# Moving the copies and picks of one-group pairs ahead of the squares of the pair before them

## The chip, the cores and the metric

The kernel runs on one core of a Trainium2 chip. The core has five engines that work side by side, each through its own queue in order: TensorE (PE, matrix products; the loading of its weights is shown as PEld), VectorE (DVE), ScalarE (ACT), GpSimd (POOL) and SyncE (SP), which here only issues transfers. They wait for each other through semaphores. The metric is the time of one execution on the device in microseconds (us); several runs are given by their median.

## The reference

A graph of 6250 nodes (128 features) and 100000 edges, sorted by destination. For each edge the features of both ends and of the edge are multiplied by a weight, normalised over the 128 outputs, cut at zero, and summed by source node; the sums are added to the nodes and normalised again:

```python
row, col = edge_index[0], edge_index[1]            # src, dst
msg_in = jnp.concatenate([x[row], x[col], edge_attr], axis=-1)
h = msg_in @ W + b
mu = jnp.mean(h, axis=-1, keepdims=True)
var = jnp.mean(jnp.square(h - mu), axis=-1, keepdims=True)
h = (h - mu) * jax.lax.rsqrt(var + LN_EPS) * gamma + beta
out = jax.ops.segment_sum(jax.nn.relu(h), row, num_segments=x.shape[0])
x = _layernorm(x + out, axis=-1)
```

## The kernel before

The nodes are split into 50 blocks by source (source modulo 50), the edges, in tiles of 128, into six splits (`SPLITS`). Two kinds of work run side by side.

*Edge work* goes over 196 quads q of four tiles. `edges` puts the product of the edge features with the weight (L589, eight instructions) and the rows of the destination (L593, four) into a bank of PSUM named hp; `evict` copies it on ACT (L601, L602) into one of eight buffers hs; `scatters` sends each tile's rows on POOL, by one indirect transfer per tile (L619), to the place in DRAM (sorted) where the edges of one source block lie together. For most quads a scatter is tied to PE: it waits until PE has come to a given place of the next quad's work. SP loads what the edges need (eT, db, win).

*Block work* takes the rows of a split back from DRAM when all its scatters have landed. It goes by pairs of blocks (`Pair`). A pair of the first four splits has two groups of three or four tiles, a pair of the fifth split (25 pairs, here numbered 100 to 124, and the last split's blocks are not among them) has one group of four tiles. A pair's steps are:

- `load_pair` (SP, L673): its rows into one of four buffers hl.
- `ones` (DVE, L691): one-hots of the edges' source nodes, ohe.
- `turn` (PE, L703): four transposes of them into the one bank tr; `turned` (ACT, L707): their copy, ohn.
- `seed` (ACT, L713): a copy of the rows into one of three PSUM banks sel.
- `pick` (PE, L730): twelve products add the source nodes' share to that bank.
- `square` (ACT, L739, L742): four squares with their sums over a row, and the root of the variance.
- `root`, `scale` (DVE, L748, L754): the reciprocal and the scaled and cut message, msg, one of two buffers.
- `sums` (PE, L763): the sums by node into the one bank pa; `add` (DVE, L771): they are added to acc.

The last split is worked on in a *tail* of 14 units of one or two pairs each (class `Unit`, the same steps with lines L799 to L870, where the rows come into the bank by a product with the unit matrix, L818), followed by the last normalisation and the output. `Unit.load` (L792) waits for the last scatter.

The order of PE, DVE, ACT and SP is written out by hand: the order in which the program emits instructions is the order of each queue. POOL's is left to the planner. A pair starts every four steps of `work`; the list `FLOW` says at which step of a pair (its offset) each of its steps is emitted, and within one step of `work` the list's own order holds:

```python
    FLOW = [(14, lambda x: x.add()), (11, second(lambda x: (x.root(1), x.scale(1)))),
            (9, lambda x: (x.root(0), x.scale(0))), (13, lambda x: x.sums()),
            (8, second(lambda x: x.pick(1))), (6, lambda x: x.pick(0)),
            (7, second(lambda x: x.seed(1))), (5, lambda x: x.seed(0)),
            (9, second(lambda x: x.square(1))), (7, lambda x: x.square(0)),
            (4, lambda x: x.turned()), (2, lambda x: x.turn()),
            (0, lambda x: x.ones()),
            (-6, None)]
```

`second` skips a step for pairs of one group. So with i for the pair that started last, ACT's order among one-group pairs is turned, seed, square of pair i-1, then the same three of pair i. PE's is sums of i-3, picks of i-1, transposes of i. Per quad q the program emits edge loads, the one-hots of quad q + 2 (DVE, L577), the products of quad q, one step of `work`, the eviction of q, and the other steps that are due (for the fifth split's pairs 25 pairs over quads 181 to 196, six or seven steps per quad). The rest of the steps, mixed with the first unit, follows behind the loop.

Of the kernel before, what the change touches and what calls it, by code (L numbers as in the profile page):

```python
# [83 lines left out]
def fast_path(ctx, tc, io, bad_d):  # L84
# [584 lines left out]
    def load_pair(s, p):  # L669

        k = 2 * SPLITS[s][1]
        pair = late["blk"].tile([P, KMAX, ROW], F32, name="hl", bufs=4)
        nc.sync.dma_start(flat(pair[:, :k, :]),  # L673
                          dram_ap(sorted_d[s], p * k * P * ROW, [[k * ROW, P], [1, k * ROW]]))
        loaded[s, p] = pair
# [274 lines left out]
    first, second = pieces[0][1], pieces[1][1]  # L950
# [62 lines left out]
    def second(step):  # L1013
        return lambda x: step(x) if len(x.groups) > 1 else None

    FLOW = [(14, lambda x: x.add()), (11, second(lambda x: (x.root(1), x.scale(1)))),
            (9, lambda x: (x.root(0), x.scale(0))), (13, lambda x: x.sums()),
            (8, second(lambda x: x.pick(1))), (6, lambda x: x.pick(0)),
            (7, second(lambda x: x.seed(1))), (5, lambda x: x.seed(0)),
            (9, second(lambda x: x.square(1))), (7, lambda x: x.square(0)),  # L1020
            (4, lambda x: x.turned()), (2, lambda x: x.turn()),
            (0, lambda x: x.ones()),
            (-6, None)]

    def work(n):

        nonlocal n_steps
        for _ in range(n):
            for off, step in FLOW:
                i = n_steps - LEAD - off  # L1030
                if i % 4 or not 0 <= i // 4 < len(pairs):
                    continue
                if step is None:
                    load_pair(*pairs[i // 4])
                    continue
                if off == 0:
                    at_work[i // 4] = Pair(*pairs[i // 4])
                step(at_work[i // 4])
            n_steps += 1
# [66 lines left out]
    units = [Unit(sum(sizes[:i]), n) for i, n in enumerate(sizes)]  # L1106
# [45 lines left out]
    work(n_tail - n_steps)  # L1152
    for i in range(3):
        units[i].load()
    work(2)
    units[3].load()
    units[0].ones()
    work(2)
    units[0].turn()
    units[0].turned()  # L1160
    work(3)
    units[0].pick(0)
    units[1].ones()
    units[0].xs_load()
    units[1].turn()
    units[0].square()
    work(4)
    assert not steps_at and not others and all(cleared[s] == NB // 2 for s in cleared)
    units[2].ones()
    units[4].load()  # L1170
# [6 lines left out]
@with_exitstack  # L1177
def gnn_resnorm_kernel(ctx, tc, io):
    nc = tc.nc
    keep = ctx.enter_context(tc.tile_pool(name="keep", bufs=1))  # L1180
    bad_t = keep.tile([1, 1], I32, name="bad_t")
    with ExitStack() as inner:
        fast_path(inner, tc, io, bad_t)
    flag = nc.values_load(bad_t[0:1, 0:1], min_val=0, max_val=1 << 20,
                          skip_runtime_bounds_check_because="a sum of small counts")
    with tc.If(flag > 0):
        with ExitStack() as inner:
            general_path(inner, tc, io)
# [233 lines left out]
```

## Time and profile before

| what | us |
|---|---|
| median of 3 runs (lowest, highest) | 1142.15 (1140.5, 1145.27) |
| the profiled execution | 1144.18 |
| its span, first to last instruction | 1142.4 |
| busy in it: PE, PEld | 874.6, 811.4 |
| busy: DVE, ACT, POOL | 841.6, 768.3, 817.1 |
| one-hot copies of one-group pairs (L707), first to last | 955.12 to 1041.42 |
| last scatter starts | 1032.22 |
| the tail's first load; unit 1's first product | 1035.83; 1049.23 |

In the rows that are shown, a line of the order of time has the start, the duration, the engine, the line of the program, the operation, what it writes and reads by the program's names, how many instructions are put together, and in brackets how long the engine had been idle and who released it. A row of the waits has who waited for whom, microseconds in total, how many times, and the longest. A row of a stage has its bounds and length, the busy time of PE, PEld, DVE, ACT and POOL with their counts, the granted clock of TensorE as a share of full speed, the share of the DMA engines, and GB/s. Matmuls are pipelined, so a group's duration reaches beyond the start of the next; the distances between starts say what a step costs PE.

### The profile page before, as it was taken

The page shows a single profiled execution, that of the slowest core. Times are in us where ns is not written, and L with a number is a line of the kernel's source. Part 1 is how long each engine was busy: PE and PEld are TensorE (multiplying, and loading weights), DVE is VectorE, ACT ScalarE, POOL GpSimd, SP SyncE. Part 2 cuts the span into 40 slices and gives each one's busy share as a digit, 9 for nine tenths or more (in the row PEclk, how much of TensorE's full clock was granted, in tenths as well). Part 3 has the DMA queues.
Part 4 walks back from the last instruction along what each step waited for, and adds up shares of the span by engine and source line. Part 5 has one row for each costly group of instructions (what it writes and reads, how often), then busy time and mean ns, then how long its engine had stood idle before and what let it go on. Part 6 is the DMA issues. An engine that isn't in the chain of part 4 may idle for free.

```text
span 1142.4 us, 27577 instructions
## 1 busy us (share of the span) xinstructions
PE 874.6 (77%) x8873; PEld 811.4 (71%) x8873; DVE 841.6 (74%) x2352; ACT 768.3 (67%) x3115; POOL 817.1 (72%) x877
## 2 busy tenths in 40 slices
PE   3668676537887869787787879888888998777993
PEld 2657565437787868787787869888887888775762
DVE  6875666236877777676868678987989887666984
ACT  3324432207676867677676778988889998776993
POOL 3677777777777777777777777777777776761675
PEclk9688887667988989899899989999999999999996
DMA  7698998457877763887786758776878676744531
GB/s 216 208 274 255 293 290 250 133 175 230 254 255 231 241 202 124 281 244 237 226 262 208 228 185 283 250 228 211 254 225 259 202 236 183 209 127 139 166 131 59
DMA packets 123539, 247.48 MB, mean 217 GB/s; under 512 B 47036, under 2 KB 55245, under 8 KB 123384
## 3 DMA queue, kind: packets, MB, share of 16 engines
q1 hardware_dynamic: 97332, 191.92, 55.0%
q0 software_dynamic: 25184, 53.31, 13.2%
q8 instruction: 71, 1.16, 0.4%
q14 instruction: 84, 0.69, 0.2%
q10 hardware_dynamic: 868, 0.40, 0.2%
HBM read 155.74 MB, written 89.80 MB: 215 GB/s over the span
## 4 chain that ended last, share of the span: by engine, by line
PE 31%; DVE 22%; DMA 22%; ACT 13%; issue 6%; POOL 4%; SPq 1%; ACTq 0%; POOLq 0%; DVEq 0%
DMA sorted<-hs,place_i 16%; PE pa L763 7%; PE sel L730 7%; PE hp L589 7%; DVE msg L754 5%; DMA db<-drel_d 4%; ACT sq L739 3%; DVE sc L437 3%; PE beside L484 3%; ACT sel L713 3%; DVE ohe L691 3%; ACT ohn L707 2%; POOL sorted L619 2%; ACT hs L601 2%; PE hp L593 2%
## 5 line engine op out<-in xcount | busy, mean ns | idle before, releaser
L619 POOL DMA_INDIRECT sorted<-hs,place_i x782 | 757.8, 969 | 253.6 <-issue 102.7
L730 PE MATMUL sel<-xa,ohn 128*128 128x128 bf16 x2550 | 188.1, 225 | 126.5 <-ACT sel L713 125.5
L730 PEld LDWEIGHTS <-ohn 128*128 128x128 bf16 x2550 | 165.4, 101 | 141.4 <-issue 111.4
L589 PE MATMUL hp<-w,eT 128*128 128x128 f32 x1564 | 241.5, 303 | 26.4 <-ACT hs L601 26.4
L739 ACT ACTIVATE sq<-sel 128x128 f32<-128x128 f32 x850 | 224.2, 281 | 47.4 <-PE sel L730 47.4
L589 PEld LDWEIGHTS hp<-w,eT 128*128 128x128 f32 x1564 | 218.8, 214 | 52.3 <-ACT hs L601 28.9
L754 DVE SCALAR_TENSOR_TENSOR msg<-sel,rstd,cut 128x128 f32<-128x128 f32 x850 | 240.7, 345 | 7.9
L601 ACT COPY hs<-hp 128x512 f32<-128x512 f32 x196 | 114.1, 582 | 195.3 <-DMA sorted<-hs,place_i 152.5
L763 PE MATMUL pa<-msg,ohe 128*128 128x130 f32 x1700 | 234.0, 291 | 3.5 <-DVE msg L754 3.0
L763 PEld LDWEIGHTS pa<-msg,ohe 128*128 128x128 f32 x1700 | 214.8, 203 | 5.3 <-DVE msg L754 4.3
L739 ACT ACTIVATION_READ_ACCUMULATOR sq<-sel 128x1 f32 x850 | 179.8, 212 | 0.0
L691 DVE TENSOR_TENSOR ohe<-hl,beside 128x1024 f32<-128x1024 f32 (+2 forms) x125 | 131.6, 1053 | 36.2 <-DMA hl<-sorted 24.5
L713 ACT COPY sel<-hl 128x512 f32<-128x512 f32 (+1 forms) x225 | 127.9, 568 | 14.4 <-DVE msg L754 14.1
L577 DVE TENSOR_SCALAR ohd<-db,part_w 128x512 bf16<-128x512 bf16 x194 | 72.1, 372 | 66.1 <-DMA db<-drel_d 41.3
L707 ACT COPY ohn<-tr 128x1024 bf16<-128x1024 bf16 (+2 forms) x125 | 108.7, 870 | 0.0
L748 DVE RECIPROCAL rstd<-std 128x4 f32<-128x4 f32 (+1 forms) x225 | 38.7, 172 | 91.1 <-ACT std L742 88.1
L593 PE MATMUL hp<-win,ohd 126*128 126x128 bf16 x782 | 82.9, 232 | 2.4 <-DMA win<-xb_d 2.4
L703 PE MATMUL tr<-ident_h,ohe 128*128 128x128 bf16 x850 | 70.4, 224 | 8.7 <-issue 7.4
L742 ACT ACTIVATE std<-ss,eps 128x4 f32<-128x4 f32 (+1 forms) x225 | 66.9, 297 | 7.3
L593 PEld LDWEIGHTS <-ohd 126*128 126x128 bf16 x782 | 66.7, 105 | 6.3 <-issue 2.6
L771 DVE TENSOR_TENSOR acc<-acc,pa 128x260 f32<-128x260 f32 x100 | 41.7, 417 | 29.4 <-PE pa L763 26.6
L703 PEld LDWEIGHTS <-ohe 128*128 128x128 bf16 x850 | 54.6, 100 | 9.4 <-issue 7.6
(193 smaller groups left out, 1038.6 us busy)
## 6 DMA issues: line engine op xcount, KB each, us to landing
eT<-in_eT SPq DMA_DIRECT2D x96, 512.0 KB
hl<-sorted SPq DMA_DIRECT2D x75, 528.0 KB
db<-drel_d SPq DMA_DIRECT2D x96, 256.0 KB
sorted<-empty SPq DMA_DIRECT2D x100, 198.0 KB
hl<-sorted SPq DMA_DIRECT2D x50, 264.0 KB
sorted<-hs,place_i POOLq DMA_INDIRECT x782
hl<-sorted SPq DMA_DIRECT2D x25, 396.0 KB
sorted<-empty SPq DMA_DIRECT2D x50, 132.0 KB
```

Of the source, the lines that this page charges most:

```text
L589: pe(nc.tensor.matmul(hp[:, j, :], eT[:, at], w[:, 2, :], start=j == 0, stop=False, skip_group_check=True), 4)
L593: pe(nc.tensor.matmul(hp[:, j, :], oh[:3 * WN, at], win[:3 * WN, :], start=False, stop=j == m - 1, skip_group_check=True))
L601: nc.scalar.copy(hs[:, :m, 0:D], hp[:, :m, :])
L619: i = nc.gpsimd.indirect_dma_start(out=sorted_d[s][:, :], out_offset=bass.IndirectOffsetOnAxis(ap=place_i[:parts, t:t + 1], axis=0), in_=h ...
L691: nc.vector.tensor_tensor(self.ohe[:, :k, :], self.hl[:, :k, D:D + 1].to_broadcast([P, k, P]), row_bc(iota_p, k), op=ALU.is_equal)
L703: pe(nc.tensor.transpose(tr[:, j, :], half[:, j0 + j, 1::2], ident_h))
L707: nc.scalar.copy(self.ohn[:, :self.k, :], self.tr[:, :self.k, :])
L713: nc.scalar.copy(self.sel[g][:, :m, :], self.hl[:, j0:j0 + m, 0:D])
L730: pe(nc.tensor.matmul(sel[:, j, :], self.ohn[:, j0 + j, :], xa[:, b, i * D:(i + 1) * D], start=False, stop=j == m - 1 and i == 2, skip_gro ...
L739: nc.scalar.activation(sq[:, j, :], self.sel[g][:, j, :], AF.Square, accum_out=ss[:, j:j + 1])
L754: nc.vector.scalar_tensor_tensor(self.msg[:, j0 + j, 0:D], self.sel[g][:, j, :], rstd[:, j:j + 1], cut, op0=ALU.mult, op1=ALU.max)
L763: pe(nc.tensor.matmul(self.pa[:, h, :], self.ohe[:, j, :], self.msg[:, j, :], start=(j == h), stop=(j == k - 2 + h)), 4)
```

## The change

For pairs with one group the copy of the one-hots and of the rows is emitted at step 3 of the pair instead of steps 4 and 5, in the list ahead of the squares (step 7, so those of the pair before fall into the same step of `work`), and its picks at step 5 instead of 6. Pairs with two groups keep their order. Behind the loop the last steps are mixed in another order with the first unit: its one-hots come one step sooner, its transposes and its copy stand ahead of the last pair's squares, its picks ahead of the last pair's scaling. Nothing else is changed.

```diff
+    def single(step):
+        return lambda x: step(x) if len(x.groups) == 1 else None
+
     FLOW = [(14, lambda x: x.add()), (11, second(lambda x: (x.root(1), x.scale(1)))),
             (9, lambda x: (x.root(0), x.scale(0))), (13, lambda x: x.sums()),
-            (8, second(lambda x: x.pick(1))), (6, lambda x: x.pick(0)),
-            (7, second(lambda x: x.seed(1))), (5, lambda x: x.seed(0)),
+            (8, second(lambda x: x.pick(1))), (6, second(lambda x: x.pick(0))),
+            (5, single(lambda x: x.pick(0))),
+            (7, second(lambda x: x.seed(1))), (5, second(lambda x: x.seed(0))),
+            (3, single(lambda x: (x.turned(), x.seed(0)))),
             (9, second(lambda x: x.square(1))), (7, lambda x: x.square(0)),
-            (4, lambda x: x.turned()), (2, lambda x: x.turn()),
+            (4, second(lambda x: x.turned())), (2, lambda x: x.turn()),
             (0, lambda x: x.ones()),
             (-6, None)]
...
     for i in range(3):
         units[i].load()
+    work(1)
+    units[0].ones()
+    units[3].load()
+    work(1)
+    units[0].turn()
+    work(1)
+    units[0].turned()
+    work(1)
+    units[0].pick(0)
+    units[0].xs_load()
+    units[1].ones()
     work(2)
-    units[3].load()
-    units[0].ones()
-    work(2)
-    units[0].turn()
-    units[0].turned()
-    work(3)
-    units[0].pick(0)
-    units[1].ones()
-    units[0].xs_load()
     units[1].turn()
     units[0].square()
-    work(4)
+    work(5)
...
     units[2].ones()
     units[4].load()
```

## The prediction

> **What bounds the kernel now.** I read the page's slices first, then busy time by stage, then the waits of the stage that the change touches, then one pair in order of time.
>
> ```profile
> span 1142.4 us, 27577 instructions
> ...
> POOL 3677777777777777777777777777777776761675
> ...
> 958.50:1024.40 65.90, 50.63 (x580) 48.06 (x579) 43.83 (x137) 50.74 (x228) 44.89 (x47) 1.00 0.58 173
> ...
> ACT sq L739 <- PE sel L730: 19.0, 23, 1.0
> ...
> 959.39 0.57 ACT L707 COPY ohn<-tr 128x512 bf16<-128x512 bf16 x1
> 1024.35 0.56 ACT L707 COPY ohn<-tr 128x512 bf16<-128x512 bf16 x1
> 1041.42 0.57 ACT L707 COPY ohn<-tr 128x512 bf16<-128x512 bf16 x1
> ```
>
> The slices (a fortieth of the span each) show POOL, which issues the scatters, at seven tenths in nearly every slice up to the 36th; towards its end the pairs with one group (25 of them, numbers 100 to 124) have their stretch. There no engine is full: in the stage row ACT is busy 50.74 of 65.90 us, PE 50.63, DVE 43.83, POOL 44.89. ACT's only wait in 958 to 1043 is the one quoted, 23 times before the first square, 19.0 us in all. The copies L707 of pairs 101, 119 and 124 stand at 959.39, 1024.35 and 1041.42: 23 periods in 82.03 us, of which the last five, without edges, take 3.41 each and the first eighteen 3.61. One period, with an eviction in it:
>
> ```profile
> 1002.69 0.57 ACT L707 COPY ohn<-tr 128x512 bf16<-128x512 bf16 x1
> 1003.16 0.59 ACT L601 COPY hs<-hp 128x512 f32<-128x512 f32 x1
> 1003.73 0.60 ACT L713 COPY sel<-hl 128x512 f32<-128x512 f32 x1
> 1004.38 0.83 PE L730 MATMUL sel<-xa,ohn 128*128 128x128 bf16 x12 [0.82 <-ACT sel L713]
> 1005.05 0.39 PE L703 MATMUL tr<-ident_h,ohe 128*128 128x128 bf16 x4
> 1005.27 1.11 PE L763 MATMUL pa<-msg,ohe 128*128 128x130 f32 x8
> 1005.31 0.28 ACT L739 ACTIVATE sq<-sel 128x128 f32<-128x128 f32 x1 [0.98 <-PE sel L730]
> 1006.22 1.05 PE L589 MATMUL hp<-w,eT 128*128 128x128 f32 x8
> 1006.69 0.57 ACT L707 COPY ohn<-tr 128x512 bf16<-128x512 bf16 x1
> 1006.81 0.18 DVE L748 RECIPROCAL rstd<-std 128x4 f32<-128x4 f32 x1 [1.73 <-ACT std L742]
> 1007.03 1.13 DVE L754 SCALAR_TENSOR_TENSOR msg<-sel,rstd,cut 128x128 f32<-128x128 f32 x4
> 1007.15 0.59 ACT L713 COPY sel<-hl 128x512 f32<-128x512 f32 x1
> 1007.67 0.59 ACT L601 COPY hs<-hp 128x512 f32<-128x512 f32 x1
> ...
> 1010.44 1.13 DVE L754 SCALAR_TENSOR_TENSOR msg<-sel,rstd,cut 128x128 f32<-128x128 f32 x4
> 1011.48 0.42 DVE L771 TENSOR_TENSOR acc<-acc,pa 128x260 f32<-128x260 f32 x1
> ```
>
> The chain is serial: copy of the one-hots (L707), copy of the rows (L713), picks on PE (L730), squares on ACT (L739), next copy. PE waits for ACT (0.82 before 1004.38), then ACT for PE (0.98 before 1005.31). An eviction (L601, 1003.16 to 1003.73) adds 0.57 when it stands between the copies and nothing when it stands behind the second (1007.67), since it falls into ACT's wait.
>
> **The change, part by part.** No instruction is added or removed; instructions change places.
>
> *1. The copies of pair i+1 ahead of the squares of pair i.* ACT's own work per pair, start to start, is 0.46 (1006.69 to 1007.15) + 0.52 (1007.15 to 1007.67) + 1.38 (1005.31 to 1006.69) = 2.36 us, against 3.41. The naive gain is 0.98 x 23, about 22 us. I don't take it, because the next wait is already in the order of PE's queue: sums (L763) of pair i-2, picks of pair i, transposes (L703) of pair i+1. That order stays, but the squares of i-2 now run behind the copies of i-1, directly ahead of the copies of i. So the sums that stand in front of the picks, and which had a full period of slack, are now late: they need the scaled messages (L754) and the bank that the add (L771) of the pair before empties, and DVE does that add behind the scaling. From the first square of pair i-1 to the first square of pair i+1, two periods, the loop is, start to start: square to reciprocal 1.50 (1005.31 to 1006.81); to scaling 0.22 (to 1007.03); to add 1.04 (1010.44 to 1011.48); to sums 0.46; to picks 0.95 (1005.27 to 1006.22, what followed the sums there); to transposes 0.67 (1004.38 to 1005.05); to the one-hot copy 0.43; to the row copy 0.46; to the square 0.52. The two links that those rows lack:
>
> ```profile
> 873.50 0.40 DVE L771 TENSOR_TENSOR acc<-acc,pa 128x260 f32<-128x260 f32 x1
> 873.96 1.89 PE L763 MATMUL pa<-msg,ohe 128*128 128x130 f32 x12 [0.36 <-DVE acc L771]
> ...
> 1047.82 0.62 PE L809 MATMUL tr<-ident_h,ohe 128*128 128x128 bf16 x8 [1.26 <-DVE ohe L799]
> 1048.48 1.01 ACT L812 COPY ohn<-tr 128x1024 bf16<-128x1024 bf16 x1 [0.41 <-PE tr L809]
> ```
>
> 873.50 to 873.96 is add to sums (PE waited for that add); the copy starts 0.04 behind the end of the transposes (1048.44), and four transposes take 0.39 (1005.05). Sum 6.25 us per two pairs, 3.13 per pair. In general, with d the time between the copies of two neighbouring pairs, the next d is the larger of 2.36 and 6.25 - d.
>
> Five periods without edges: 5 x 3.13 = 15.6 us. Two things cost nothing as long as their cover holds. The row copy of pair i+1 takes the bank (one of three) of pair i-2, whose scaling ends a period earlier; were it late, the squares would queue behind the copy on ACT. DVE's own work is about 2.4 per pair (one-hots, reciprocal, scaling, add, a part of a slot's edge one-hots), so it has 0.7 to spare.
>
> *2. Edges in that loop.* ACT's evictions now always fall between squares and the next copy: 2.36 + 0.57 = 2.93, under 3.13. The products of a slot cost PE 0.95 + 0.23 = 1.18:
>
> ```profile
> 1012.10 1.11 PE L589 MATMUL hp<-w,eT 128*128 128x128 f32 x8
> 1013.05 0.39 PE L593 MATMUL hp<-win,ohd 126*128 126x128 bf16 x4
> 1013.27 1.11 PE L763 MATMUL pa<-msg,ohe 128*128 128x130 f32 x8
> ```
>
> In ten of the twelve slots (edge quads 184 to 195, six or seven steps each) they stand between transposes and sums, where PE waits for the add; there they only demand d of at least 0.22 - 0.43 + 1.18 + 0.95 + 0.67 + 0.43 = 3.02. In two, 190 and 192, whose first step is two steps behind a pair's start, they stand between picks and transposes, inside the loop, and the eviction waits for them: PE's products end 0.67 + 0.95 + 0.39 behind the picks' start, then 0.04 and 0.57, so the copy comes 2.62 behind the picks where it came 1.10, 1.52 more. Stepping d with these rules from pair 101 gives 3.2, then 3.06 and 3.20 in turn up to pair 110, then 4.7, 2.37, 3.9, 3.9, 2.4, 3.8, 2.4, 3.8 to pair 119: 58.7 us for eighteen, where 18 x 3.13 would be 56.3. With part 1: 58.7 + 15.6 = 74.3 against 82.03, gain 7.7.
>
> *3. The beginning.* The first pair's picks had stood behind the products of 956.02, at 957.14; now they stand ahead of them, behind the sums of 954.62, so at 956.02 at the earliest (1.40 later, as the products did).
>
> ```profile
> 954.62 1.56 PE L763 MATMUL pa<-msg,ohe 128*128 128x130 f32 x12
> 956.02 1.05 PE L589 MATMUL hp<-w,eT 128*128 128x128 f32 x8
> 957.14 0.83 PE L730 MATMUL sel<-xa,ohn 128*128 128x128 bf16 x12
> ```
>
> The products then start at 956.7, the transposes at 957.9, the eviction (0.57) follows the products, and the copy of pair 101 comes at 958.5 for 959.39: gain 0.9. The row copy of pair 100 waits for a bank of pair 98 (scaled until 954.8): 0.4 us, hidden behind the same picks.
>
> *4. The tail's entry.* Unit 0's one-hots, transposes, copy and picks move ahead of the last pairs' scaling and squares. Measured from the copy of pair 124, before it is 7.81 us to unit 1's first matmul (1041.42 to 1049.23). After: sums of 122 and picks of 124 at 2.15, unit 0's transposes at 2.82, its copy at 3.3, squares of 124 at 3.75; DVE has unit 1's one-hots (1.22, from 4.2) ahead of that reciprocal, so the scaling starts at 5.6, the add 1.04 later, sums 0.46 later at 7.1, unit 1 at 8.05. Loss 0.2. This needs unit 0's one-hots on DVE (0.68) no later than 2.1 behind the copy, at about 1034.7, which hangs on the scatters:
>
> ```profile
> L619 POOL DMA_INDIRECT sorted<-hs,place_i x54: 867/965/992, 958.0 to 1032.2; - x54
> ...
> 1030.95 0.97 POOL L619 DMA_INDIRECT sorted<-hs,place_i  x1 [0.30 <-ACT sq L739]
> 1032.22 0.87 POOL L619 DMA_INDIRECT sorted<-hs,place_i  x1 [0.30 <-issue]
> 1035.83 7.47 SPq L792 DMA_DIRECT2D hl<-sorted  x7
> 1042.81 0.68 DVE L799 TENSOR_TENSOR ohe<-hl,beside 128x512 f32<-128x512 f32 x1
> 1049.23 1.02 PE L818 MATMUL sel<-hl,ident 128*128 128x512 f32 x2
> ...
> 670.95 0.34 SPq L673 DMA_DIRECT2D hl<-sorted  x1
> 675.21 1.22 DVE L691 TENSOR_TENSOR ohe<-hl,beside 128x1024 f32<-128x1024 f32 x1 [4.01 <-DMA hl<-sorted]
> ```
>
> Unit 0's load waits for the last scatter: 3.61 us from its start to the load. The 54 scatters from 958.0 run at 1.27 where nothing holds them (1030.95 to 1032.22); 53 x 1.27 = 67.3, so the last starts at 1025.3 at best, and I take 1026.5, since slots of 5.1 us (6.25 steps of a pair's four, at 3.25 per pair) just feed four scatters of 1.27. The load goes at 1030.1 and lands within 4.3 (670.95 to 675.21, for twice the bytes): 1034.4. It just fits. SP's loads wait for row copies, which all come earlier, and land two periods ahead of their use: nothing. Unit 1's transposes and unit 0's squares now stand behind the scaling of 124 on their queues' lists, and DVE, not they, is what unit 1 waits for: nothing.
>
> The tail behind unit 1 has the same instructions in the same order and moves as a whole.
>
> **Sum.** 0.9 + 7.7 - 0.2 = 8.4 us off. The profiled execution took 1144.18 (span 1142.4 and 1.8 around it), 2.03 above the median of 1142.15. So 1135.8 for such an execution, 1133.7 as a median. 0.5% of this kernel, 5.7 us, is about what a measurement can tell from no change.
>
> The Trainium skill's Perfetto Trace Analysis, section Engine Utilization, says that in a well-optimized kernel at least one engine should approach full utilization; by it the loop would close up to ACT's own work, which is the first rival below. The stage row, 50.74 of 65.90, doesn't show that yet.
>
> **Rivals.**
>
> *ACT alone bounds* (the sums don't hold the picks). For it: wherever sums follow at once (1005.27) DVE was done. Against it: PE did wait for the add at 873.96. Then pair 124 is through early and unit 0's rows decide: 1025.3 + 3.61 + 4.3 = 1033.2 for its one-hots, 9.6 ahead of 1042.81; that is 1142.15 - 9.6 = 1132.5, or 1131.5 if half the bytes land a us sooner. Chance 0.15.
>
> *The scatters don't come forward*: they are tied to PE's progress and POOL has little to spare. Then the one-hots come at 1035.83 + 4.3 = 1040.1, and unit 1 follows about 6.4 later as before (1042.81 to 1049.23), at 1046.5: 2.7 us gained, 1139.4. Each us of the last scatter later than 1026.5 costs one. For it: of the 74.2 us from the first of the 54 to the last, 67.3 are POOL's own pace. Against it: the other 6.9 are waits behind a PE that now runs ahead. Chance 0.2. The Trainium skill's SBUF — State Buffer, section SBUF: two separate sides, says that certain VectorE operations lock GpSimd out of a shared port so that it can't write descriptors; a denser DVE would then slow the scatters. Here they last 867 to 992 ns with DVE busy 43.83 of 65.90 us, which shows no such loss.
>
> *Slower: the products stand in the loop in every slot*, because they are held there (rows or windows of the edges late, or DVE's one-hots for them behind the new scaling). Its place is between picks and transposes, its price 1.52 per slot: 12 x 1.52 = 18.2 for the 2.4 counted, 15.8 more, 1149.5. It decides from a mean period of 3.57 (82.03 / 23), that is from some five more slots than my two. Against it: PE had no wait for edge data in this stretch. Chance 0.08.
>
> *The wait only moves* from squares to copies, the period stays about 3.4: 0 to 2 us gained, 1141. Chance 0.07.
>
> **How the numbers follow.** My forecast has 0.5; its own range is 1131.5 to 1136.5. The range of 1130.5 to 1140.5 takes in the second and third case and leaves out the slower one and half of the last. Faster by over 0.5% (below 1136.4): the ACT case and nearly all of the forecast, 0.64; within: the scatter case, the moved wait and the forecast's edge, 0.28; slower 0.08.
>
> **What would show it.** ACT's wait for picks falls from 19.0 us to under 5; in its place come waits of the one-hot copies for transposes, some 0.77 x 23 = 15 to 18 us, and of the sums for the add. The copies of 101 and 124 stand near 958.5 and 1032.8, the last scatter near 1026.5, unit 0's load near 1030, unit 1's first matmul near 1041, and from there to the end as many us as before. It is wrong if the mean period is under 2.9 or over 3.4, or if unit 0's one-hots wait for their rows.

## The result, and the profile after

The changed kernel takes 1136.28 us (median of 8 runs, 1132.87 to 1138.08), the kernel before beside it 1143.51 (8 runs, 1140.5 to 1146.59): a ratio of 0.993, 95% interval 0.991 to 0.995. That is 7.2 us off, inside the predicted range and 2.6 us above the predicted 1133.7. The profiled execution took 1132.87, the lowest of its eight, with a span of 1131.1.

Its page, the span and POOL's slices, and three stages (bounds and length; busy time and count of PE, PEld, DVE, ACT, POOL; clock; DMA share; GB/s): from the copy of pair 101 to that of 119, on to that of 124, and from unit 1's first product to the end.

```profile
span 1131.1 us, 27553 instructions
...
POOL 3677777777777777777777777777777776772675
```

```profile
955.20:1014.30 59.10, 50.03 (x570) 46.70 (x569) 42.77 (x138) 50.09 (x222) 44.33 (x46) 1.00 0.63 192
1014.30:1029.70 15.40, 10.80 (x126) 9.73 (x125) 10.21 (x33) 12.48 (x58) 7.83 (x9) 1.00 0.43 132
1037.99:1131.10 93.11, 69.69 (x626) 52.77 (x624) 70.24 (x282) 68.34 (x333) 54.70 (x52) 0.90 0.35 115
```

The same work of ACT (50.09 us; 50.74 before) and of PE (50.03; 50.63) now stands in 59.1 us, where the stage shown of before has 65.9 (64.96 from copy to copy). POOL goes on at seven tenths in nearly every slice. The marks in the order of time:

```profile
955.20 0.59 ACT L707 COPY ohn<-tr 128x512 bf16<-128x512 bf16 x1
...
1014.31 0.58 ACT L707 COPY ohn<-tr 128x512 bf16<-128x512 bf16 x1 [0.66 <-PE tr L703]
...
1023.71 0.86 POOL L619 DMA_INDIRECT sorted<-hs,place_i  x1 [0.30 <-issue]
...
1025.85 5.73 SPq L792 DMA_DIRECT2D hl<-sorted  x7
...
1029.69 0.58 ACT L707 COPY ohn<-tr 128x512 bf16<-128x512 bf16 x1 [0.26 <-PE tr L703]
...
1031.05 0.68 DVE L799 TENSOR_TENSOR ohe<-hl,beside 128x512 f32<-128x512 f32 x1
...
1037.99 1.02 PE L818 MATMUL sel<-hl,ident 128*128 128x512 f32 x2
```

The 23 periods take 74.49 us (1029.69 less 955.20) for 82.03. Pair 99's copy, which stands ahead of everything the change touches, starts at 947.38, where it started at 950.81: 3.43 us of the 11.3 between the two spans are a difference of the two executions and not of the change. From that copy to unit 1's first product it is 98.42 before and 90.61 after, 7.81 us less; from there to the end 93.2 and 93.1. So the 7.8 us are all in the stretch that the change touches, which fits the 7.2 of the medians.

The waits of the stretch from 940 to 1035 (who waited for whom, us in total, times, longest):

```profile
PE pa L763 <- DVE acc L771: 15.0, 18, 1.7
...
ACT ohn L707 <- PE tr L703: 8.2, 12, 1.1
...
PE sel L730 <- ACT sel L713: 1.3, 4, 0.6
```

ACT's wait for picks, 19.0 us before, has left the list. In its place PE waits for the add ahead of the sums, and ACT for the transposes ahead of the copies. The chain that ended last shows why these two belong together. One turn of it, two pairs long (start, length, what; the short pieces between are left out):

```profile
962.61 1.08 ACT sq L739 x8
...
964.25 1.13 DVE msg L754 x4
965.38 0.34 DVE acc L771
...
965.76 1.16 PE pa L763 x8
966.92 0.67 PE sel L730 x12
967.59 0.24 PE tr L703 x4
...
967.85 0.02 ACT ohn L707
967.88 0.46 issue
968.34 0.60 ACT sel L713
968.93 1.07 ACT sq L739 x8
```

Squares, scaling, add, sums, picks, transposes, copy of the one-hots, row copy, squares of the pair after the next: 6.32 us, 3.16 per pair. What the chain calls "issue" is the time behind the start of the copy of the one-hots, which runs then (0.58 us from 967.85).

### The profile page after: what moved, and what is told of

Read it like the earlier page. It is cut to its first block, busy times and chain, and to the rows that moved or that the text cites. A ratio compares the mean times of both kernels' runs of the same rounds, so it can differ in the third digit from the quotient of the medians.

```text
span 1131.1 us, 27553 instructions
## 1 busy us (share of the span) xinstructions
PE 875.0 (77%) x8873; PEld 808.9 (72%) x8873; DVE 841.0 (74%) x2352; ACT 767.1 (68%) x3115; POOL 816.4 (72%) x877
## 3 DMA queue, kind: packets, MB, share of 16 engines
q8 instruction: 71, 1.16, 0.4%
## 4 chain that ended last, share of the span: by engine, by line
PE 31%; DVE 23%; DMA 20%; ACT 13%; issue 7%; POOL 5%; SPq 1%; ACTq 0%; POOLq 0%; DVEq 0%
DMA sorted<-hs,place_i 15%; PE pa L763 8%; PE hp L589 8%; PE sel L730 6%; DVE msg L754 5%; DMA db<-drel_d 4%; PE beside L484 4%; ACT sq L739 3%; DVE sc L437 3%; ACT sel L713 3%; POOL sorted L619 3%; DVE ohe L691 2%; ACT hs L601 2%; PE hp L593 2%; ACT sc L459 2%
## 5 line engine op out<-in xcount | busy, mean ns | idle before, releaser
L763 PEld LDWEIGHTS pa<-msg,ohe 128*128 128x128 f32 x1700 | 211.6, 200 | 24.9 <-DVE acc L771 20.3
```

Of the source, the lines that this page charges most:

```text
L763: pe(nc.tensor.matmul(self.pa[:, h, :], self.ohe[:, j, :], self.msg[:, j, :], start=(j == h), stop=(j == k - 2 + h)), 4)
```

## The experiments

All of them are edits of the changed kernel, except where the old list is kept. One went to a chip like the first. The others went to two other chips, on which the kernel before itself takes 1390 us; what that means is shown ahead of them, since it decides what they can say.

**The late sums.** For one-group pairs the sums go two steps back in the list and the add two steps, so that the picks of the next pair stand ahead of them in PE's queue:

```diff
-    FLOW = [(14, lambda x: x.add()), (11, second(lambda x: (x.root(1), x.scale(1)))),
-            (9, lambda x: (x.root(0), x.scale(0))), (13, lambda x: x.sums()),
+    FLOW = [(16, single(lambda x: x.add())), (15, single(lambda x: x.sums())),
+            (14, second(lambda x: x.add())), (11, second(lambda x: (x.root(1), x.scale(1)))),
+            (9, lambda x: (x.root(0), x.scale(0))), (13, second(lambda x: x.sums())),
...
-    work(5)
+    work(7)
```

> The later sums once more, to see whether they run on a chip on which the kernel before takes about 1143 us, since the first eight kernels ran on one where it takes 1390. If it does: by the loop theory 23 periods in 61 to 66 us instead of the changed kernel's 74.5, no wait of the sums for the add, unit 0's one-hots waiting for their rows, ratio to before 0.989 to 0.992; by the rival, that ACT or PE itself bounds, periods of 74 us and 0.993. On the slower chip: 0.994 again, with PE idle by issue in the periods.

Measured: 1133.98 us (6 runs, 1133.75 to 1136.12) beside 1144.38 of the kernel before (11 runs), ratio 0.9913, interval 0.9899 to 0.9928. Two stages of its profile (101 to 119, 119 to 124), and the order of time at its tail's entry:

```profile
957.58:1011.18 53.60, 48.71 (x562) 45.25 (x561) 43.09 (x136) 49.70 (x223) 40.80 (x43) 1.00 0.68 207
1011.18:1024.46 13.28, 11.17 (x128) 9.79 (x128) 10.90 (x35) 12.50 (x58) 10.24 (x11) 1.00 0.34 100
```

```profile
1024.46 0.59 ACT L707 COPY ohn<-tr 128x512 bf16<-128x512 bf16 x1 [0.25 <-PE tr L703]
...
1025.17 0.87 POOL L619 DMA_INDIRECT sorted<-hs,place_i  x1 [0.30 <-issue]
...
1027.32 3.17 SPq L792 DMA_DIRECT2D hl<-sorted  x7
...
1030.19 0.69 DVE L799 TENSOR_TENSOR ohe<-hl,beside 128x512 f32<-128x512 f32 x1 [4.28 <-DMA hl<-sorted]
...
1039.02 1.02 PE L818 MATMUL sel<-hl,ident 128*128 128x512 f32 x2
```

The 23 periods take 66.88 us, 7.6 less than with the change and 15.2 less than before (a little above the 61 to 66 that were expected; why is read below, under ACT's own work); in the stretch from 935 to 1035 no row of the list has PE waiting for the add for more than 0.3 us. So the sums in front of the picks, waiting for the add, are what sets the changed kernel's period: shown by taking them out of the way. What comes next is what the first rival said would follow: the pairs run ahead of POOL, whose scatters follow each other at 1.28 us (56 from 954.7 to 1025.2), the last stands behind the last copy instead of 6 us ahead, and unit 0's one-hots wait 4.28 us for their rows. From pair 99's copy (949.75 in this profile) to unit 1's first product it is 89.27 us, 1.34 better than the change, although the pairs are 7.6 us faster. This version is the fastest that was measured, by its median; its interval overlaps that of the change.

**The two other chips.** The changed kernel again, with nothing edited:

> The changed kernel as it is, for comparison with the three others on the same chip: ratio to before 0.993 as measured already.

Measured: 1389.34 us for 1389.29 of the kernel before, ratio 0.9991, interval 0.9966 to 1.0015: no gain to be seen. A row of the waits of the whole profile, then places in the order of time, down to the last copies of the one-group pairs:

```profile
PE sel L730 <- issue: 76.5, 99, 3.4
```

```profile
1212.40 0.39 PE L703 MATMUL tr<-ident_h,ohe 128*128 128x128 bf16 x4
...
1216.90 0.58 ACT L707 COPY ohn<-tr 128x512 bf16<-128x512 bf16 x1 [3.25 <-PE pa L763]
...
1220.66 0.41 DVE L771 TENSOR_TENSOR acc<-acc,pa 128x260 f32<-128x260 f32 x1
...
1221.13 2.10 PE L763 MATMUL pa<-msg,ohe 128*128 128x130 f32 x8 [1.95 <-issue]
...
1277.01 0.58 ACT L707 COPY ohn<-tr 128x512 bf16<-128x512 bf16 x1 [0.56 <-PE tr L703]
...
1280.31 0.58 ACT L707 COPY ohn<-tr 128x512 bf16<-128x512 bf16 x1 [0.82 <-PE tr L703]
...
1283.33 0.58 ACT L707 COPY ohn<-tr 128x512 bf16<-128x512 bf16 x1 [0.55 <-PE tr L703]
...
1286.63 0.58 ACT L707 COPY ohn<-tr 128x512 bf16<-128x512 bf16 x1 [0.82 <-PE tr L703]
```

PE is idle again and again with no releaser named ("issue"), in all 76.5 us ahead of picks alone, where the first chip's profile of the same program has 0.2. The label by itself doesn't show that nothing held PE: the sums of 1221.13, with 1.95 us of "issue", start 0.06 behind the end of the add of 1220.66, which they wait for as in the loop. What the rows do show is that, by the profile's times, PE's results reach ACT late. The copy of 1216.90 starts 4.1 us behind the end of its transposes (1212.40 and 0.39), with ACT idle for 3.25 of them, where the first chip mostly has 0.03 from end to copy. Over the 23 periods, 101.22 us there, ACT's waits ahead of copies and evictions come to 39.0 us, for 11.3 on the first chip; that is about what the periods are longer by (26.7). Why the results come late isn't shown; such places are called stops below. They are not everywhere: the last four periods are 3.03, 3.30, 3.02 and 3.30, two of them 6.32, as on the first chip. So the ratios from these chips say little about the loop (only the one-hots alone came out there at the ratio that was expected), and the shortest two neighbouring periods of a profile say much: they are the loop where no stop fell.

| kernel | chip of the first kind or other | ratio to before, interval | 23 periods, us | shortest two neighbouring, us |
|---|---|---|---|---|
| before | first | 1 | 82.03 | 6.82 |
| after | first | 0.993 [0.991, 0.995] | 74.49 | 6.32 |
| late sums | first | 0.9913 [0.9899, 0.9928] | 66.88 | 5.27 |
| old list, new entry of the tail | other | 0.9979 [0.9955, 1.0002] | 104.53 | 6.83 |
| one-hots only | other | 1.0012 [0.9992, 1.0032] | 105.08 | 7.17 |
| one-hots only, again | other | 1.0011 [0.9992, 1.0031] | 112.57 | 7.17 |
| after | other | 0.9991 [0.9966, 1.0015] | 101.22 | 6.32 |
| new list, old entry of the tail | other | 1.0008 [0.9987, 1.0029] | 101.62 | 6.32 |
| transposes sooner | other | 0.9988 [0.9969, 1.0007] | 100.40 | 6.33 |
| transposes sooner, again | other | 0.9978 [0.9961, 0.9995] | 103.42 | 6.32 |
| add first | other | 0.9961 [0.9935, 0.9986] | 101.67 | 5.52 |
| late sums | other | 0.9943 [0.9913, 0.9974] | 97.87 | 5.27 |
| late sums, transposes sooner | other | 0.9948 [0.9917, 0.9979] | 98.07 | 5.27 |
| late sums, tail behind | other | 0.9963 [0.9945, 0.9982] | 94.32 | 5.28 |

The last column is the same for a list wherever it ran. In the five profiles that have the new list with the sums and the add where the change leaves them, no two neighbouring periods take less than 6.32.

**The list alone.** The new list with the old entry of the tail:

```diff
-    work(1)
-    units[0].ones()
-    units[3].load()
-    work(1)
-    units[0].turn()
-    work(1)
-    units[0].turned()
...
+    work(2)
+    units[3].load()
+    units[0].ones()
+    work(2)
+    units[0].turn()
+    units[0].turned()
```

> The new order of steps in the list, with the order of the tail's entry as before the change. Theory of the loop (squares, scaling, add, sums, picks, transposes; two pairs in 6.25 us): the copies L707 of pairs 101 to 124 take about 74.5 us as with the whole change, and the way from the copy of 124 to unit 1's first product about 8.9 us (unit 1's transposes wait for its one-hots, which stand behind an add, and the sums of 124 stand behind them) against 8.30 with the whole change: 0.3 to 1 us slower than the whole change, a ratio to before of about 0.994. Rival, that the tail's new order brings a good part of the gain: the ratio goes back to 0.997 or more.

Measured: 1390.52 us, 1.0008, and two periods of 6.32 as with the whole change. From the copy of pair 124 to unit 1's first product it is 9.04 us, with the change on that chip 7.94.

**The tail's entry alone.** The old list with the new entry, unit 3's load one step later:

```diff
-            (8, second(lambda x: x.pick(1))), (6, second(lambda x: x.pick(0))),
-            (5, single(lambda x: x.pick(0))),
-            (7, second(lambda x: x.seed(1))), (5, second(lambda x: x.seed(0))),
-            (3, single(lambda x: (x.turned(), x.seed(0)))),
+            (8, second(lambda x: x.pick(1))), (6, lambda x: x.pick(0)),
+            (7, second(lambda x: x.seed(1))), (5, lambda x: x.seed(0)),
...
-            (4, second(lambda x: x.turned())), (2, lambda x: x.turn()),
+            (4, lambda x: x.turned()), (2, lambda x: x.turn()),
...
     units[0].ones()
-    units[3].load()
     work(1)
+    units[3].load()
```

> The old list with the new order of the tail's entry (unit 3's load one step later than in the change, since the rows' copy of pair 124 comes later in the old list). Loop theory: the 23 periods stay at 82.0 us and the entry takes about 8.0 us where it took 7.8: ratio 1.000, within 0.1%. Rival that the tail's order brings the gain: 0.996 or less.

Measured: 1388.19 us, 0.9979, periods as before (6.83 for two), and 6.26 us from the copy of pair 124 to unit 1's first product in its profile. With the old list the new entry seems to shorten that distance (7.81 before, but on the first chip), with the new list it is 1.1 us shorter than the old entry's 9.04, by one profile each. The list, and not the tail, carries the periods.

**Only the one-hots ahead.** The rows and the picks stay at their old steps, and unit 3's load comes one step later:

```diff
-            (8, second(lambda x: x.pick(1))), (6, second(lambda x: x.pick(0))),
-            (5, single(lambda x: x.pick(0))),
-            (7, second(lambda x: x.seed(1))), (5, second(lambda x: x.seed(0))),
-            (3, single(lambda x: (x.turned(), x.seed(0)))),
+            (8, second(lambda x: x.pick(1))), (6, lambda x: x.pick(0)),
+            (7, second(lambda x: x.seed(1))), (5, lambda x: x.seed(0)),
+            (3, single(lambda x: x.turned())),
...
     units[0].ones()
+    work(1)
     units[3].load()
-    work(1)
```

> Only the copy of the one-hots moves ahead of the squares of the pair before; the rows' copy stays at step 5 and the picks at step 6, so the rows' copy now stands behind the squares on ACT. Loop theory, with the order of ACT one-hot copy, squares of the pair before, rows' copy: picks wait for the rows' copy, so one period is 0.46 + 1.38 + 0.59 + 0.05 + 0.67 + 0.43 = 3.58 us without edges, nothing gained on 3.41: the 23 periods take 83 to 86 us, ratio 1.001 to 1.004, and ACT's wait is for transposes. Rival that the one-hot copy alone frees PE: periods near 3.1, ratio 0.994.

> Only the copy of the next pair's one-hots stands ahead of the squares; its rows and its picks stay where they were. Theory (PE's order: sums, picks, transposes): the squares now queue behind a copy that needs transposes, which stand behind the picks, so the loop is transposes 0.67 behind the picks, copy 0.43, squares 0.52, row copy 1.38, picks 0.60: 3.6 us per pair. 23 periods 83 to 86 us (before 82.0), ratio to before 1.001 to 1.004. Rival (the copy alone takes its 0.46 us out of ACT's chain): period 2.95 and some 70 us, ratio 0.990.

Measured: 1.0012 and 1.0011. A period of the first of the two profiles in which no stop fell, in the order of time:

```profile
1285.00 0.58 ACT L707 COPY ohn<-tr 128x512 bf16<-128x512 bf16 x1 [1.14 <-PE tr L703]
...
1285.48 0.28 ACT L739 ACTIVATE sq<-sel 128x128 f32<-128x128 f32 x1
...
1286.86 0.58 ACT L713 COPY sel<-hl 128x512 f32<-128x512 f32 x1
...
1287.49 0.83 PE L730 MATMUL sel<-xa,ohn 128*128 128x128 bf16 x12 [1.20 <-ACT sel L713]
...
1288.16 0.39 PE L703 MATMUL tr<-ident_h,ohe 128*128 128x128 bf16 x4
...
1288.58 0.58 ACT L707 COPY ohn<-tr 128x512 bf16<-128x512 bf16 x1 [1.14 <-PE tr L703]
```

Copy to squares 0.48, to the row copy 1.38, to the picks 0.63, to the transposes 0.67, to the next copy 0.42: 3.58 us, with ACT idle 1.14 for the transposes each time. Twelve of the 46 periods of the two profiles are 3.58 or 3.59, none is shorter. The rival with 2.95 falls. A copy that goes ahead of the squares alone brings nothing, because the squares then queue behind a copy that waits for transposes that wait for picks; rows and picks have to go with it. That holds by the order of the queues; the ratio itself can't tell 1.001 from 1.

**Transposes sooner.** The whole change, and a one-group pair's transposes one step earlier, so that no products can stand between its picks and them:

```diff
-            (4, second(lambda x: x.turned())), (2, lambda x: x.turn()),
+            (4, second(lambda x: x.turned())), (2, second(lambda x: x.turn())),
+            (1, single(lambda x: x.turn())),
```

> The whole change, and the transposes of one-group pairs emitted at step 1 instead of 2, directly behind the picks, so that in no slot the edges' products stand between picks and transposes. Loop theory: the two slots whose products stood in the loop (the periods of 4.53 and 3.96 us from pairs 111 and 114 on) shrink to 3.0 to 3.8, the eighteen periods with edges take 56.5 to 57.5 us instead of 59.1, 1 to 2.4 us off the whole change's time, ratio 0.991 to 0.993. Rival, that those long periods come from the scatters or from edge data that are late: they stay.

> The whole change, and the transposes of a one-group pair one step sooner, so that no slot's products can stand between its picks and its transposes. Theory (products inside the loop in two slots, 1.52 us each): the two long periods (4.53 behind pair 111 and 3.96 behind pair 114) go, the first eighteen periods take 56.5 to 57.5 us for 59.1, the last five stay at 15.4; ratio 0.991 to 0.993. Rival (the long periods have another cause, such as DVE's one-hots for the edges): 59 us as with the change, ratio 0.993.

Measured: 0.9988 and 0.9978, inside or at the edge of what the change itself gave there (0.9966 to 1.0015). The period behind pair 111 is 4.44 and 4.07 in the two profiles, 4.10 with the change on that chip, among stops of a microsecond and more: this did not tell the two theories apart. What the two long slots are is read below from the first chip's profiles.

**The add first.** The add of a pair ahead of the next pair's scaling in DVE's list, the sums in their place:

```diff
-    FLOW = [(14, lambda x: x.add()), (11, second(lambda x: (x.root(1), x.scale(1)))),
-            (9, lambda x: (x.root(0), x.scale(0))), (13, lambda x: x.sums()),
+    FLOW = [(13, single(lambda x: x.sums())), (13, single(lambda x: x.add())),
+            (14, second(lambda x: x.add())), (11, second(lambda x: (x.root(1), x.scale(1)))),
+            (9, lambda x: (x.root(0), x.scale(0))), (13, second(lambda x: x.sums())),
```

> The whole change, and for one-group pairs the add L771 of the pair before emitted ahead of the scaling instead of behind it, nothing else. Loop theory, with the add and its bank as the link: the sums no longer wait for scaling plus add, only for the messages, and the loop loses about 0.95 of its 6.25 us, 2.65 per pair; with edges the floor is 3.0 in a slot's period. The 23 periods take 62 to 68 us instead of 74.5 and the wait of the sums for the add goes (15 us before). The time gains less than that, since the last scatter, which starts at 1023.7 with the whole change, can come at most some 2 us earlier, and unit 0's rows then decide: 1 to 4 us off the whole change, ratio 0.990 to 0.992. Rival, that ACT or PE itself bounds the periods of 3.1: they stay at 74 us.

Measured: 0.9961, and the shortest two periods, in one place, 5.52 where the change has 6.32. This takes the other link out of the same ring (scaling to add, 1.13 in the chain above) and opens it too. Over the whole stretch, 101.67 us among the stops, nothing is to be seen of it.

**Late sums there.** The late sums by the edit shown above, and the same with the edit of the transposes:

> The whole change, and for one-group pairs the sums and the add two steps later (15 and 16 instead of 13 and 14), so that the sums that stand ahead of the picks of pair i are those of pair i-3 instead of i-2. Loop theory: the loop then spans three pairs and no longer binds; ACT's own 2.36 us and 2.93 with an eviction do, or 3.0 with a slot's products: 23 periods in 61 to 66 us instead of 74.5, no wait of the sums. The last pair's sums and add come later behind the others by less than a us. Unit 0's rows decide the rest: 1 to 4 us off the whole change, ratio 0.990 to 0.992. Rival, that ACT or PE itself bounds: the periods stay.

> Later sums and transposes at step 1 together: the periods under 64 us. If unit 0's rows (last scatter) bound behind them, the time is the same as with the later sums alone within 0.5 us, and unit 0's one-hots show a wait for their rows; if the pairs still bound, another 1 to 2 us go.

Measured: 0.9943 and 0.9948, 97.87 and 98.07 us for the 23 periods, 5.27 for the shortest two in both. Even among the stops the late sums gain more than the change (0.9991), by 0.5%, with intervals that just touch; the transposes add nothing to it.

**The tail behind.** The late sums, and unit 0's steps behind the last pair's scaling and sums (the new order; the lines that it replaces are left out):

```diff
+    work(1)
+    units[3].load()
+    work(8)
+    units[0].ones()
+    work(3)
+    units[0].turn()
+    units[0].turned()
+    units[0].pick(0)
+    units[0].xs_load()
+    units[1].ones()
+    units[1].turn()
+    units[0].square()
+    work(1)
```

> The late sums again, and unit 0's one-hots, transposes, copy and picks behind the last pair's scaling and sums, so that nothing of the last pairs queues behind rows that the scatters hold back. Theory (with the sums late, ACT bounds and then unit 0's rows decide): 23 periods 66 to 67.5 us as with the late sums alone, the last scatter about 0.7 us behind the copy of pair 124, unit 0's one-hots 5.0 us behind that scatter, and unit 1's first product 10.0 to 11.5 us behind the copy of pair 124 where it came 14.6 behind; median 1130 us (1129 to 1131.5), ratio 0.986 to 0.989. Rival (unit 1 has to wait for its own rows or for unit 0's work, not for the last pairs'): no earlier product, 1134 us, ratio 0.991.

Measured: 1386.18 us, 0.9963, interval 0.9945 to 0.9982. On that chip the last scatter starts at 1263.76, 9.8 us ahead of the copy of pair 124 (1273.59), so the condition that it was made for, rows that come late, isn't there. Unit 1's first product comes 9.17 us behind that copy, 8.11 with the late sums on the other of the two chips. So where the rows are in time the order seems to cost 1.06 us, by one profile each; what it does where they are late was not measured.

## Why the prediction was right

**The loop.** It named the ring of two pairs that takes the place of ACT's wait, 6.25 us, and took 3.13 per pair instead of the 2.36 that ACT's own work would give. The ring measures 6.32, link by link: square to scaling 1.64 (forecast 1.72), to add 1.13 (1.04), to sums 0.38 (0.46), to picks 1.16 (0.95), to row copy 1.42 (1.56), to square 0.59 (0.52). The five periods without edges take 15.38 us (15.6), the first eighteen 59.11 (58.7). That the sums hold the picks was argued from the order of PE's queue; the late sums show it.

**ACT's own work.** It was put at 2.36 us a pair and 0.57 for an eviction, and both held. The late sums' profile, at a place where ACT waits for nothing:

```profile
1003.18 0.28 ACT L739 ACTIVATE sq<-sel 128x128 f32<-128x128 f32 x1
...
1004.56 0.56 ACT L601 COPY hs<-hp 128x512 f32<-128x512 f32 x1
...
1005.12 0.58 ACT L707 COPY ohn<-tr 128x512 bf16<-128x512 bf16 x1
```

The squares run 1.38 us to the next instruction, the eviction 0.56; from the copy to the row copy it is 0.48 and to the squares 0.52. What was wrong is the size of the new wait: the copies wait 8.2 us for transposes, forecast 15 to 18. The 0.77 x 23 behind that forecast leaves out the twelve evictions, which fill 6.8 us of this time by the prediction's own 0.57. With them its 74.3 us leave 13.2 in which ACT doesn't work, and the measured 74.5 leave 13.4, of which 8.2 are these waits, 2.4 waits of evictions (read below) and the rest short ones. The loop and its time are not touched by this. In the late sums' 66.88 us the same working leaves 5.8: ACT there is near its own work, not at it.

**Edges.** Of the ten slots that only demand 3.02 the rule was right in the sum and not in the single periods: d_next = 6.25 - d gives no reason for equal halves, and they come as 2.52 and 3.81, 3.02 and 3.30, 2.62 and 3.71, where 3.06 and 3.20 was forecast. The two slots with the products inside the loop are there, behind pair 111 (4.53, forecast 4.7) and behind 114 (3.96, forecast 3.9). The first, in the order of time:

```profile
988.74 0.83 PE L730 MATMUL sel<-xa,ohn 128*128 128x128 bf16 x12
...
989.41 1.11 PE L589 MATMUL hp<-w,eT 128*128 128x128 f32 x8
...
990.36 0.39 PE L593 MATMUL hp<-win,ohd 126*128 126x128 bf16 x4
...
990.59 0.39 PE L703 MATMUL tr<-ident_h,ohe 128*128 128x128 bf16 x4
...
990.78 0.58 ACT L601 COPY hs<-hp 128x512 f32<-128x512 f32 x1 [1.48 <-DMA sorted<-hs,place_i]
...
991.36 0.59 ACT L707 COPY ohn<-tr 128x512 bf16<-128x512 bf16 x1
```

The copy comes 2.62 us behind the picks, to the hundredth what the step had, and 1.10 behind where no products stand between (985.73 to 986.83). The profile puts the eviction's idle time of 1.48 down to a scatter that empties its buffer, and the chain that ended last goes through that scatter too. The products end at 990.75, 0.03 ahead of the eviction. Other rows say that they set it. From 860 us on, nine evictions of the three profiles from the first kind of chip have a wait listed; all nine start 0.03 or 0.04 behind the end of the products, whichever of the two is named. In the second slot the products are named:

```profile
1001.08 0.58 ACT L601 COPY hs<-hp 128x512 f32<-128x512 f32 x1 [0.91 <-PE hp L593]
```

They are named in both slots of the late sums as well (evictions at 989.94 and 999.22), and in these three places too the copy comes 2.62 behind the picks. So the rival that scatters make the long periods has little left.

**The beginning** gained 0.76 us (forecast 0.9): the copies of 99 and 101 are 7.82 apart for 8.58.

**The tail's entry** lost 0.49 (forecast 0.2): 8.30 us from the copy of 124 to unit 1's first product. The picks of 124 come 2.49 behind its copy, not 2.15, because the period before it is a short half (2.74) of the ring, and the sums of 122 therefore wait longer for their add. The links behind hold: scaling at 5.79 (5.6), add at 6.83, sums at 7.30 (7.1). On the other chip the new list with the old entry took 1.1 us longer there (9.04 for 7.94), by one profile each: the edit of the tail seems to pay even though the distance grew.

**The scatters** came forward as the forecast wanted. The last starts at 1023.71, 1027.1 by the kernel before's count (3.43 more), forecast 1026.5. "It just fits" was too careful: the load goes 2.14 us behind the last scatter, not 3.61, and rows land 2.87 behind their load (1027.32 to 1030.19 in the late sums' profile), not 4.3. So unit 0's rows were there about 2.3 us ahead of its one-hots at 1031.05, which did not wait. Here two misses offset each other: with the forecast's own 7.9 us from the last scatter to the rows they would have come at 1035.0, 0.3 later than the entry allows, so that they cost nothing was in part luck. What late rows cost is seen with the late sums: unit 1 comes 14.56 us behind the copy of pair 124 there, 6.26 more than with the change, with one-hots that wait 4.28 for their rows. The scatters themselves did not become slower with a denser DVE (42.77 of 59.10 us busy, 43.83 of 65.90 before): 55 of them in the stretch have a median of 967 ns, 965 before. The lock of a shared port that the Trainium skill's SBUF — State Buffer, section SBUF: two separate sides, tells of shows no more here than it did there.

**The sum.** By the prediction's terms: 0.76 for 0.9, 5.85 and 1.69 for 6.3 and 1.5 in the periods, -0.49 for -0.2, in all 7.81 for 8.4. The medians differ by 7.2, so the gain is 1.2 of the 2.6 us between forecast and median. The other 1.4 are the point it started from: the kernel before's median was 1142.15 over three runs and is 1143.51 over eight.

**The rivals.** "ACT alone bounds" fell for the change. For the late sums what it said of the end came true: unit 0's rows decide, and unit 1's first product is 9.15 us nearer to pair 99's copy than before, where that case had 9.6; of ACT itself it is nearly so, with 5.8 us of waits in 66.88. By the rule of the Trainium skill's Perfetto Trace Analysis, section Engine Utilization, that one engine should approach full utilization, that kernel comes closer: in its first stage ACT is busy 49.70 of 53.60 us, after the change 50.09 of 59.10. "The wait only moves" was half true: it moved, into a ring that is 0.5 us per two pairs shorter than the old one. "Slower" needed products in the loop in every slot; they were there in two.

## What to carry to other kernels

When a wait between two engines is taken out by moving work forward, write down the next ring through all queues, start to start, before counting the gain; here it gave 6.25 us against a measured 6.32, where the engine's own work promised more than twice the gain. Look in each in-order queue for what now stands in front of the moved step and has lost its slack: the sums, harmless before, had to go behind the picks as well. Where a profile is disturbed, the shortest stretches show the ring that the mean hides. And check a releaser that the profile names by the end times: evictions put down to a scatter started 0.03 us behind the end of the products, as did those put down to products.

## What the hardware showed that was not expected

Two of the chips run the same program in 1390 us where others take 1143, with PE idle at "issue" in many places (for the picks 76.5 us in 99 waits, 0.2 us in one on the first chip) and, in the stretch of the one-group pairs, with ACT's waits ahead of copies and evictions grown from 11.3 to 39.0 us, while the last 93 us, from unit 1's first product to the end, take as long as on the first (92.9 and 93.1). There the gain of the change is not measurable (0.9991, 0.9966 to 1.0015), though the undisturbed periods show it. What makes the stops on those chips was not found; in the stretch of the one-group pairs the granted clock is lower too, 0.93 and 0.78 in the two stages below where the first chip has 1.00, which can be a cause or a consequence of the stops.

```profile
1185.41:1263.81 78.40, 55.54 (x575) 51.29 (x574) 43.01 (x137) 50.28 (x222) 46.28 (x48) 0.93 0.50 146
1263.81:1286.63 22.82, 11.18 (x112) 10.00 (x112) 9.77 (x32) 12.68 (x58) 5.96 (x7) 0.78 0.32 93
```
